# Pools laid in another order at two stage boundaries, and a last projection that ends token tile by token tile

## The chip, the cores and the metric

The kernel runs on one core of a Trainium2 chip. The metric is the device time of one execution in microseconds (us), the median of three runs.

## What is computed

Three layers with residuals over x of 512 tokens (8 batches of 64) and 512 features, all in float32. Cut to what matters:

```python
x = x + xattn(layernorm(x), ctx)      # 32 query heads, 8 key heads, 1601 keys per batch
x = x + mixer(layernorm(x))           # state space layer: 8 groups of 8 heads
x = x + routed(layernorm(x))          # top 1 of 8 experts, rank 16

# xattn: q, k rms-normed per head
out = softmax(q @ k.T * scale + mask) @ v          # per head
return out.reshape(B, Q, 32 * 128) @ o_proj_w.T    # the last projection

# mixer
dt = softplus(h @ w_dt + bias); dA = exp(-dt * exp(A_log))
xBC = silu(conv4(h @ w_in)); state = state * dA + dt * x * B; y = state @ C + x * D
return (groupnorm(y) * silu(h @ w_gate)) @ out_proj_w.T
```

## The kernel before

The work is written with tiles from pools. A pool holds so many buffers for each tag; pools are stacked in SBUF (and banks in PSUM) in the order in which they are opened, and when a stage closes its pools, the next stage's pools take the same addresses. An instruction that writes a tile waits for those that still use a pool that lay there. A scheduler orders the instructions of each engine by priority; within an engine they run in that order. All DMAs are issued by one queue, SP.

**Queries** (`project_queries`, L148). The layer norm of x, then 16 pairs of query heads in Strassen-like blocks (L199). Each quad of heads is scaled by its norm's factors (`finish`, L251, q_st) and stored to DRAM (L260, q_d). Its pools stand above the pools of context and weights: big, weights, wk2, small, late; q_raw, the factors and q_st lie in late, the topmost.

**Attention** (`attend_all`, L298). 32 units (8 batches by 4 pairs of key heads). For each unit, PE makes keys (`keys`, L375, banks a to d; evacuated into kT by ACT at L365 and DVE at L367), values (`values`, L435, into v) and, for the unit before, scores (L495), which DVE scales and masks (L500), maxima, exponentials and outputs (L565). The list `order` (L622) weaves the nine pieces of a unit's projections with the unit before's attention. Its pools are wk2, small, k, attn, v in SBUF, and two PSUM pools: ps2 with two score banks, ps1 with a, b, c, d, tr and av.

**Last projection** (`last_projection`, L669). Woven with the last unit's attention. 32 heads are taken in 16 pieces of 2; `prefetch` loads a piece's weights and attention outputs (`spare`, into the buffers of the context, a ring of four), and `piece` multiplies them for four token tiles into banks a to d (po_a to po_d). The last batches' outputs come late: for pieces 12 to 15, token tile 3 is left out (L695), and `rest` (L709) first adds po_a to po_c to x, then does these eight products for po_d with outputs loaded into o_last, and adds po_d.

**Mixer** (`mixer_and_routed`, L905). The first w_in load (L957), a layer norm with transposes for each token tile (L963, one bank px) and the products for dt (pdt, L965). A chain of small operations over [128, 256] (sp_z at L972 to a at L993) makes dt and a. For each group, `steps` (L1006, POOL) makes av from a, `decay` (L1017) multiplies it on PE (seg) and ACT takes the exponential; `project` (L1024, pj, four products for each of ten column blocks) goes through DVE's convolution (L1035, L1041) and ACT. Groups overlap: the mixing of a group (pg L1062, px, py) stands among the projections of the next. The routed layer follows at the end.

What decides the order around the change: `tc.issue_after` for ACT's table switches, the list at L1203, and else the scheduler's priorities, which by default follow the order of the text.

## Time and profile before

| what | us |
|---|---|
| median of three runs | 2874.32 (2873.58, 2874.32, 2877.37) |
| the profiled execution, its own time | 2875.87 |
| its span (first to last instruction) | 2874.1 |
| PE busy | 2815.8 |
| DVE, POOL, ACT busy | 1724.0, 834.0, 724.0 |
| first keys on PE (L375) | from 128.75 |
| first scores (L495) | from 182.77 |
| last product of the last projection (L718) | to 2345.95 |
| first projection of the mixer (L1024) | from 2356.45 |
| first mixing on PE, which begins group 1 (L1062) | 2400.66 |
| a unit of attention; a group of the mixer | 64.98; 60.1 |

How to read it: times are microseconds from the start of the span. A matmul instruction in float32 shows as two records. In a timeline row the columns are start, length, engine, line, operation, tiles, shape and count; the bracket holds the engine's idle time before the row and what ended it. PE is busy almost throughout, so the places of interest are those where it stands or where the granted TensorE clock is below 1.

### The profile page before, as it was taken

The page shows a single profiled execution, that of the slowest core. Times are in us where ns is not written, and L with a number is a line of the kernel's source. Part 1 is how long each engine was busy: PE and PEld are TensorE (multiplying, and loading weights), DVE is VectorE, ACT ScalarE, POOL GpSimd, SP SyncE. Part 2 cuts the span into 40 slices and gives each one's busy share as a digit, 9 for nine tenths or more (in the row PEclk, how much of TensorE's full clock was granted, in tenths as well). Part 3 has the DMA queues.
Part 4 walks back from the last instruction along what each step waited for, and adds up shares of the span by engine and source line. Part 5 has one row for each costly group of instructions (what it writes and reads, how often), then busy time and mean ns, then how long its engine had stood idle before and what let it go on. Part 6 is the DMA issues. An engine that isn't in the chain of part 4 may idle for free.

```text
span 2874.1 us, 37794 instructions
## 1 busy us (share of the span) xinstructions
PE 2815.8 (98%) x14716; PEld 2011.2 (70%) x14716; DVE 1724.0 (60%) x3013; ACT 724.0 (25%) x1282; POOL 834.0 (29%) x786
## 2 busy tenths in 40 slices
PE   8899999999999999999999999999999999999997
PEld 7677787777777777777777777777777544444444
DVE  4546666576667666756766676666665325445544
ACT  3222223222222222222222222222222103222221
POOL 4314323322222322232222232223222215334430
PEclk9999999999999999999999999999999999999998
DMA  4821322232113122221311222223113341121100
GB/s 162 286 61 45 85 73 52 53 93 52 45 47 93 46 63 67 73 60 45 96 49 45 66 73 60 50 68 84 46 34 89 119 160 37 52 91 64 52 15 15
DMA packets 276571, 205.89 MB, mean 72 GB/s; under 512 B 155084, under 2 KB 239882, under 8 KB 275370
## 3 DMA queue, kind: packets, MB, share of 16 engines
q1 hardware_dynamic: 276394, 203.49, 24.8%
q8 instruction: 117, 1.92, 0.3%
q14 instruction: 60, 0.49, 0.1%
HBM read 180.82 MB, written 22.62 MB: 71 GB/s over the span
## 4 chain that ended last, share of the span: by engine, by line
PE 89%; DVE 4%; DMA 3%; issue 2%; POOL 1%; ACT 0%; SPq 0%; POOLq 0%; ACTq 0%; DVEq 0%
PE pav L565 12%; PE psc L495 11%; PE pj L1024 9%; PE pv_a L435 6%; PE pv_b L435 6%; PE pv_c L435 6%; PE pk_c L375 5%; PE pk_a L375 5%; PE pk_b L375 5%; PE pv_d L435 3%; PE mo L1128 3%; PE pk_d L375 3%; PE pvl L456 2%; PE psn L404 2%; DMA nbs<-max_d 2%
## 5 line engine op out<-in xcount | busy, mean ns | idle before, releaser
L500 DVE SCALAR_TENSOR_TENSOR attn<-psc,rk,mask_sb 128x256 f32<-128x256 f32 (+1 forms) x832 | 363.7, 474 | 242.9 <-PE psc L495 225.0
L549 POOL TENSOR_TENSOR sm<-attn 128x512 f32<-128x512 f32 x64 | 81.9, 1280 | 1143.5 <-ACT attn L547 1143.5
L565 PE MATMUL pav<-attn,v 128*128 128x256 f32 (+1 forms) x1664 | 380.3, 379 | 0.0
L495 PE MATMUL psc<-q,kT 128*128 128x256 f32 x1536 | 371.2, 381 | 0.0
L552 POOL TENSOR_TENSOR sm<-sm,attn 128x512 f32<-128x512 f32 x256 | 340.0, 1328 | 29.4 <-DVE attn L543 10.7
L565 PEld LDWEIGHTS pav<-attn,v 128*128 128x128 f32 (+1 forms) x1664 | 313.9, 190 | 45.5 <-issue 1.0
L495 PEld LDWEIGHTS psc<-q,kT 128*128 128x128 f32 x1536 | 286.3, 190 | 82.0 <-issue 35.4
L1024 PE MATMUL pj<-mx_xnT,w_in 128*128 128x512 f32 x640 | 292.6, 601 | 0.0
L543 DVE TENSOR_TENSOR attn<-attn,nb 128x1024 f32<-128x1024 f32 x192 | 224.8, 1216 | 67.1 <-ACT nb L540 66.6
L435 PEld LDWEIGHTS pv_a<-wv,cx 128*128 128x128 f32 x1536 | 196.8, 192 | 58.6 <-issue 42.0
L435 PE MATMUL pv_a<-wv,cx 128*128 128x128 f32 x1536 | 214.2, 280 | 9.8 <-ACT kT L365 9.8
L547 ACT ACTIVATE attn<-attn 128x1024 f32<-128x1024 f32 x192 | 202.5, 1058 | 72.6 <-DVE attn L543 70.1
L1024 PEld LDWEIGHTS pj<-mx_xnT,w_in 128*128 128x128 f32 x640 | 118.9, 191 | 135.0 <-issue 132.9
L511 DVE TENSOR_TENSOR mx<-mx,attn 128x512 f32<-128x512 f32 x256 | 211.7, 827 | 2.0
L375 PE MATMUL pk_a<-cx,wk 128*128 128x417 f32 (+1 forms) x512 | 193.3, 500 | 0.8 <-ACT qrs L109 0.8
L386 ACT ACTIVATE ksq<-kT 128x834 f32<-128x834 f32 (+1 forms) x128 | 108.9, 871 | 161.2 <-DVE kT L367 161.2
L1132 DVE SCALAR_TENSOR_TENSOR x<-mo,rs,x 128x512 f32<-128x512 f32 x32 | 24.0, 751 | 184.6 <-PE mo L1128 184.5
L606 POOL TENSOR_TENSOR o<-o,f 128x512 f32<-128x512 f32 x31 | 39.4, 1272 | 323.7 <-DMA f<-sums_d 291.6
L375 PEld LDWEIGHTS pk_a<-cx,wk 128*128 128x128 f32 x512 | 97.2, 190 | 46.1 <-issue 20.8
L1128 PE MATMUL mo<-w_out,y 128*128 128x512 f32 x256 | 122.9, 613 | 0.0
L540 ACT COPY nb<-nbs 128x256 f32<-128x256 f32 x64 | 24.1, 376 | 324.7 <-DMA nbs<-max_d 324.7
L1041 DVE SCALAR_TENSOR_TENSOR acc<-pj,small_consts,acc 128x504 f32<-128x504 f32 x144 | 104.6, 727 | 1.0
(208 smaller groups left out, 4274.5 us busy)
## 6 DMA issues: line engine op xcount, KB each, us to landing
wk<-in_wk SPq DMA_DIRECT2D x32, 512.0 KB
wv<-in_wv SPq DMA_DIRECT2D x32, 512.0 KB
w_in<-in_w_in SPq DMA_DIRECT2D x16, 1024.0 KB
wvs<-wv_s_d SPq DMA_DIRECT2D x28, 512.0 KB
wks<-wk_s_d SPq DMA_DIRECT2D x28, 512.0 KB
cx<-in_ctxT SPq DMA_DIRECT2D x16, 834.0 KB
cx<-in_ctxT SPq DMA_DIRECT2D x16, 768.0 KB
wq<-in_wq SPq DMA_DIRECT2D x16, 512.0 KB
```

The lines of the kernel that those rows point to most:

```text
L375: nc.tensor.matmul(ps[:, :w], lhsT=u.wk[l][:, dc, :], rhs=u.cx.r[ch][r][:, dc, :], start=start and dc == 0, stop=dc == 1, skip_group_check ...
L386: nc.scalar.activation(sq[ch][:, :, half, :w], u.kT[:, :, half, lo:hi], AF.Square)
L435: nc.tensor.matmul(ps[:, i * HD : (i + 1) * HD], lhsT=u.cx.r[ch][r][:, dc, i * P : (i + 1) * P], rhs=u.wv[l][:, dc, :], start=start and i ...
L495: nc.tensor.matmul(ps[:rows, t - t2, :], lhsT=lhsT, rhs=qh, start=True, stop=True)
L500: nc.vector.scalar_tensor_tensor(out=s.at[:rows, t, :].rearrange("p (h q) -> p h q", h=GQ), in0=ps[:rows, t - t2, :].rearrange("p (h q) -> ...
L511: nc.vector.tensor_tensor(s.mx2, s.mx2, s.at[:, t2 : t2 + 2, :], ALU.max)
L543: nc.vector.tensor_tensor(at[:, k : k + 4, :], at[:, k : k + 4, :], nb.unsqueeze(1).to_broadcast([P, 4, 256]), ALU.add,)
L547: nc.scalar.activation(at[:, k : k + 4, :], at[:, k : k + 4, :], AF.Exp)
L552: nc.gpsimd.tensor_tensor(sm2, sm2, at[:, i : i + 2, :], ALU.add)
L565: nc.tensor.matmul(s.av[:, 0, :], lhsT=u.v[:rows, t, hh, :], rhs=s.at[:rows, t, :], start=t == 0, stop=t == NKT - 1,)
L1024: nc.tensor.matmul(pj, lhsT=G.w[:, dc, n, :], rhs=xnT[:, dc, :], start=dc == 0, stop=dc == DC - 1)
L1128: nc.tensor.matmul(po, lhsT=G.y[:, n, tt * P : (tt + 1) * P], rhs=G.wo[:, n, :], start=n == 0, stop=n == GC - 1,)
```

## The change

It has three parts.

Pools of attention: o, mx2, mx, nbs, sm2, sm, rbs and f move from the pool wk2, which stands below the key pool, to the attn pool above it, so that the key pool lies 18 KB lower. The two v buffers become two pools, one below attn and one above. In PSUM, tr and av move to a pool ps3 between the score banks and a to d.

Last projection: each piece multiplies all four token tiles, with o_last in place of the late outputs for tile 3 of pieces 12 to 15 (`load_newest` is called before the pieces that are left). The last two pieces are done in `rest`, token tile by token tile; after each tile's products its sum goes to x, and the scheduler's priority at that point is kept in `done`.

Mixer: the pools are opened in the order groups, weights, big; banks pj and y1 move to a pool of their own; the layer norm of token tile tt is given the priority of `done[tt]`.

```diff
 def attend_all(...):
+    vp = [ctx.enter_context(tc.tile_pool(name="xa_v0", bufs=1))]
     ap_ = ctx.enter_context(tc.tile_pool(name="xa_attn", bufs=2))
-    vp = ctx.enter_context(tc.tile_pool(name="xa_v", bufs=2))
+    vp.append(ctx.enter_context(tc.tile_pool(name="xa_v1", bufs=1)))
     ps2 = ctx.enter_context(tc.tile_pool(name="xa_ps2", bufs=2, space=PSUM))
+    ps3 = ctx.enter_context(tc.tile_pool(name="xa_ps3", bufs=1, space=PSUM))
     ps1 = ctx.enter_context(tc.tile_pool(name="xa_ps1", bufs=1, space=PSUM))
...
-        u.v = vp.tile([P, NKT, 2, HD], F32, tag="v", name="v")
+        u.v = vp[u.n % 2].tile([P, NKT, 2, HD], F32, tag="v", name="v")
...
-            psn = ps1.tile([P, 512], F32, tag="tr", name="psn")
+            psn = ps3.tile([P, 512], F32, tag="tr", name="psn")
...
-        u.o = wk2.tile([P, PQ, S], F32, tag="o", name="o")
+        u.o = ap_.tile([P, PQ, S], F32, tag="o", name="o")
...
     def last_projection():
+        def product(i, tt):
+            w, o, late = held[i]
+            for j in range(2):
+                h = 2 * i + j
+                if late and tt == NTT - 1:
+                    lhsT = newest[0][:, h - (HQ - PQ), :]
+                else:
+                    lhsT = o[:, j, tt * P : (tt + 1) * P]
+                nc.tensor.matmul(po[tt], lhsT=lhsT, rhs=w[:, j, :], start=h == 0, stop=h == HQ - 1)
+
         def piece(i):
-            w, o, late = held[i]
...
-            for j in range(2):
-                for tt in range(NTT - 1 if late else NTT):
...
+            for tt in range(NTT):
+                product(i, tt)
...
-        def rest():
+        def load_newest():
             last = loads.last_outputs()
             nc.sync.dma_start(
                 out=last.rearrange("p h (b q) -> p h b q", b=2), in_=o_d[NPR - 1][:, :, B - 2 :, :]
             )
-            for tt in range(NTT - 1):
-                add(tt)
-            for k in range(PQ):
...
-            add(NTT - 1)
+            newest.append(last)
+
+        def rest():
+            done = []
+            for tt in range(NTT):
+                for i in (HQ // 2 - 2, HQ // 2 - 1):
+                    product(i, tt)
+                nc.vector.tensor_tensor(x[:, tt, :], x[:, tt, :], po[tt], ALU.add)
+                done.append(tc.tile_snap_priority())
+            return done
...
 def mixer_and_routed(ctx, tc, c, x, done, w_in, w_out, w_ra, b_w, out):
+    grpp = ctx.enter_context(tc.tile_pool(name="mx_grp", bufs=2))
+    wst = ctx.enter_context(tc.tile_pool(name="mx_w", bufs=2))
     big = ctx.enter_context(tc.tile_pool(name="mx_big", bufs=1))
-    wst = ctx.enter_context(tc.tile_pool(name="mx_w", bufs=2))
-    grpp = ctx.enter_context(tc.tile_pool(name="mx_grp", bufs=2))
...
+    ps4 = ctx.enter_context(tc.tile_pool(name="mx_ps4", bufs=1, space=PSUM))

     def bank(tag, shape, name, bufs=1):
-        return ps.tile(shape, F32, tag=tag, name=name, bufs=bufs)
+        return (ps4 if tag in ("pj", "y1") else ps).tile(shape, F32, tag=tag, name=name, bufs=bufs)
...
-        layernorm_T(nc, c, small, ps, x, tt, xnT[:, :, tok], tag="px", bufs=2, pbufs=1, copy=nc.scalar.copy)
+        with tc.high_priority(offset=tc.tile_snap_priority() - done[tt]):
+            layernorm_T(
+                nc, c, small, ps, x, tt, xnT[:, :, tok], tag="px", bufs=2, pbufs=1, copy=nc.scalar.copy
+            )
```

More of the change, by code (lines that the diff above doesn't have):

```diff
@@ L483, in score @@
                 s.at = ap_.tile([P, NKT, 256], F32, tag="attn", name="attn")
-                s.mx2 = wk2.tile([P, 2, 256], F32, tag="mx2", name="mx2", bufs=1)
+                s.mx2 = ap_.tile([P, 2, 256], F32, tag="mx2", name="mx2", bufs=1)
             qh = u.q[:, hh * GQ : (hh + 1) * GQ, :].rearrange("p h q -> p (h q)")
@@ L516, in maxima @@
             at, lr = s.at, key_rows(NKT - 1)
-            mx = wk2.tile([P, 256], F32, tag="mx", name="mx")
+            mx = ap_.tile([P, 256], F32, tag="mx", name="mx")
             nc.vector.tensor_tensor(mx, s.mx2[:, 0, :], s.mx2[:, 1, :], ALU.max)
             nc.vector.tensor_tensor(mx[:lr], mx[:lr], at[:lr, NKT - 1, :], ALU.max)
-            tp = ps1.tile([P, 2, P], F32, tag="tr", name="mtp")
+            tp = ps3.tile([P, 2, P], F32, tag="tr", name="mtp")
             for i in range(2):
@@ L531, in maxima @@
             nc.sync.dma_start(out=row.rearrange("(i a q) -> a i q", i=2, q=32), in_=turned[0:P:32])
-            s.nbs = wk2.tile([P, 256], F32, tag="nbs", name="nbs")
+            s.nbs = ap_.tile([P, 256], F32, tag="nbs", name="nbs")
             marks["load"] = nc.sync.dma_start(out=s.nbs, in_=row.rearrange("(o q) -> o q", o=1).broadcast_to([P, 256]))
@@ L537, in softmax @@
             at, lr = s.at, key_rows(NKT - 1)
-            nb = ps1.tile([P, 256], F32, tag="tr", name="nb")
+            nb = ps3.tile([P, 256], F32, tag="tr", name="nb")
             nc.scalar.copy(nb, s.nbs)
-            sm2 = wk2.tile([P, 2, 256], F32, tag="sm2", name="sm2", bufs=1)
+            sm2 = ap_.tile([P, 2, 256], F32, tag="sm2", name="sm2", bufs=1)
             for k in range(0, NKT - 1, 4):
@@ L554, in softmax @@
             marks["exp"] = nc.scalar.activation(at[:lr, NKT - 1, :], at[:lr, NKT - 1, :], AF.Exp)
-            s.sm = wk2.tile([P, 256], F32, tag="sm", name="sm")
+            s.sm = ap_.tile([P, 256], F32, tag="sm", name="sm")
             nc.gpsimd.tensor_tensor(s.sm, sm2[:, 0, :], sm2[:, 1, :], ALU.add)
@@ L561, in outputs @@
             if part == 0:
-                s.av = ps1.tile([P, 2, 256], F32, tag="av", name="pav")
+                s.av = ps3.tile([P, 2, 256], F32, tag="av", name="pav")
             for t in range(0, 6) if part == 0 else range(6, NKT):
@@ L574, in outputs @@
                 nc.tensor.matmul(rb, lhsT=c.ones, rhs=s.sm, start=True, stop=True)
-                rbs = wk2.tile([P, 256], F32, tag="rbs", name="rbs")
+                rbs = ap_.tile([P, 256], F32, tag="rbs", name="rbs")
                 nc.vector.reciprocal(rbs, rb)
@@ L592, in sums @@
                 )
-            rbs = wk2.tile([P, 256], F32, tag="rbs", name="rbs")
+            rbs = ap_.tile([P, 256], F32, tag="rbs", name="rbs")
             nc.vector.reciprocal(rbs[:64], rb[:64])
             nc.sync.dma_start(out=u.rows.sums, in_=rbs[0:64:32])
-            u.f = wk2.tile([P, 512], F32, tag="f", name="f", bufs=1)
+            u.f = ap_.tile([P, 512], F32, tag="f", name="f", bufs=1)
             nc.sync.dma_start(
@@ L626, in attend_all @@
         u = Unit()
+        u.n = n
         u.b, u.pr = divmod(n, NPR)
@@ L669, in last_projection @@
     def last_projection():
-        po, held = [], []
+        po, held, newest = [], [], []
         def load(i):
@@ L688, in load @@
             return w, o, late
+        def product(i, tt):
[7 more added lines that the diff above has]
+                nc.tensor.matmul(po[tt], lhsT=lhsT, rhs=w[:, j, :], start=h == 0, stop=h == HQ - 1)
         def piece(i):
-            w, o, late = held[i]
             if not po:
                 po.extend(ps1.tile([P, D], F32, tag=k, name=f"po_{k}") for k in "abcd")
-            for j in range(2):
-                for tt in range(NTT - 1 if late else NTT):
-                    h = 2 * i + j
-                    nc.tensor.matmul(
-                        po[tt], lhsT=o[:, j, tt * P : (tt + 1) * P], rhs=w[:, j, :],
-                        start=h == 0, stop=h == HQ - 1,
-                    )
-        def add(tt):
-            nc.vector.tensor_tensor(x[:, tt, :], x[:, tt, :], po[tt], ALU.add)
+            for tt in range(NTT):
+                product(i, tt)
         def prefetch():
@@ L713, in rest @@
             )
-            for tt in range(NTT - 1):
-                add(tt)
-            for k in range(PQ):
-                h = HQ - PQ + k
-                nc.tensor.matmul(
-                    po[NTT - 1], lhsT=last[:, k, :], rhs=held[h // 2][0][:, h % 2, :],
-                    start=False, stop=h == HQ - 1,
-                )
-            add(NTT - 1)
-        return prefetch, [lambda i=i: (prefetch(), piece(i)) for i in range(HQ // 2)], rest
-    prefetch, last_pieces, rest = last_projection()
+            newest.append(last)
[7 more added lines that the diff above has]
+            return done
+        return prefetch, [
+            lambda i=i: (prefetch(), piece(i)) for i in range(HQ // 2 - 2)
+        ], load_newest, rest
+    prefetch, last_pieces, load_newest, rest = last_projection()
     before = divide = None
@@ L754, in attend_all @@
                 att[what]()
+        if not u:
+            load_newest()
         for piece in pieces[at:]:
@@ L757, in attend_all @@
         before = u
-    rest()
+    return rest()
 class Loads:
@@ L899, in load_mask, with mixer_and_routed @@
             nc.sync.dma_start(out=mask_sb[: KV - full * P, full, :], in_=maskT[full * P :, :])
-        attend_all(tc, c, x, loads, mask_sb, load_mask, q_d, o_d, rows_d, wo, queries_loaded)
+        return attend_all(tc, c, x, loads, mask_sb, load_mask, q_d, o_d, rows_d, wo, queries_loaded)
 @with_exitstack
-def mixer_and_routed(ctx, tc, c, x, w_in, w_out, w_ra, b_w, out):
+def mixer_and_routed(ctx, tc, c, x, done, w_in, w_out, w_ra, b_w, out):
     nc = tc.nc
+    grpp = ctx.enter_context(tc.tile_pool(name="mx_grp", bufs=2))
+    wst = ctx.enter_context(tc.tile_pool(name="mx_w", bufs=2))
     big = ctx.enter_context(tc.tile_pool(name="mx_big", bufs=1))
-    wst = ctx.enter_context(tc.tile_pool(name="mx_w", bufs=2))
-    grpp = ctx.enter_context(tc.tile_pool(name="mx_grp", bufs=2))
     wk = ctx.enter_context(tc.tile_pool(name="mx_wk", bufs=2))
@@ L1266, in perceiver @@
     c = make_consts(nc, cpool, small)
-    cross_attention(tc, c, x, ctxT, maskT, wq, wk, wv, wo)
-    mixer_and_routed(tc, c, x, w_in, w_out, w_ra, b_w, out)
+    done = cross_attention(tc, c, x, ctxT, maskT, wq, wk, wv, wo)
+    mixer_and_routed(tc, c, x, done, w_in, w_out, w_ra, b_w, out)
 def kernel(**inputs):
```

## The prediction

> **What bounds the kernel now.** I read the chain that ended last, then the timeline at the two places where one stage's pools follow another's, then the busy time by stretches there. The page's chain:

> ```profile
> PE 89%; DVE 4%; DMA 3%; issue 2%; POOL 1%; ACT 0%; SPq 0%; POOLq 0%; ACTq 0%; DVEq 0%
> ```

> The end is set by PE nearly everywhere (busy 2815.8 of 2874.1 us). So an edit counts where PE stands, runs at half clock, or gets more work. Boundary 1, from queries to attention, in the timeline:

> ```profile
> 136.27 1.63 PEld L435 LDWEIGHTS pv_d<-wvs,cs 128*128 128x128 f32 x12
> ...
> 141.84 0.36 SPq L260 DMA_DIRECT2D q_d<-q_st  x1
> ...
> 147.27 0.56 DVE L367 TENSOR_TENSOR kT<-t,pk_c 128x384 f32<-128x384 f32 x1 [5.46 <-DMA q_d<-q_st]
> 147.38 0.48 ACT L365 COPY kT<-pk_a 128x384 f32<-128x384 f32 x1 [16.51 <-DMA q_d<-q_st]
> ...
> 147.91 0.80 PE L435 MATMUL pv_a<-wv,cx 128*128 128x128 f32 x2 [9.81 <-ACT kT L365]
> ```

> The first keys stand finished in PSUM from about 134, but nobody may copy them into kT until the last queries' store, issued at 141.84, has read its tile; PE stands 9.81 us. The busy time by stretches (third to last column: the granted clock) shows what follows:

> ```profile
> 142.00:146.00 4.00, 0.00 (x0) 0.00 (x0) 0.00 (x0) 0.00 (x0) 0.00 (x0) 0.61 0.81 238
> ...
> 150.00:152.00 2.00, 2.00 (x7) 1.39 (x7) 0.56 (x1) 0.05 (x1) 1.84 (x3) 0.50 0.00 0
> ```

> The clock is halved until about 153. Boundary 2, from the last projection to the mixer:

> ```profile
> 2345.95 0.69 DVE L703 TENSOR_TENSOR x<-x,po_d 128x512 f32<-128x512 f32 x1 [3.36 <-PE po_d L718]
> ...
> 2345.99 2.54 SPq L940 DMA_DIRECT2D w_in<-in_w_in  x4
> ...
> 2346.69 0.66 PE L132 MATMUL ln_tp<-ident,ln_xn 128*128 128x128 f32 x4 [0.78 <-DVE x L703]
> ...
> 2354.69 1.97 PE L965 MATMUL pdt<-small_consts,mx_xnT 128*128 128x64 f32 x8 [0.68 <-ACT mx_xnT L133]
> 2356.45 12.18 PE L1024 MATMUL pj<-mx_xnT,w_in 128*128 128x512 f32 x22
> 2356.70 0.42 DVE L972 TENSOR_TENSOR sp_z<-pdt,small_consts 128x256 f32<-128x256 f32 x1 [6.48 <-PE pdt L965]
> ...
> 2366.89 8.04 POOL L1006 TENSOR_TENSOR av<-a,upto 128x512 f32<-128x512 f32 x8 [1.58 <-DVE a L993]
> ...
> 2368.47 3.75 PE L1017 MATMUL seg<-av,past 128*128 128x512 f32 x8
> ```

> After the last product (call T = 2345.95 its end) come four small rounds of transposes and pdt, 10.5 us, then pj. The clock is halved again from 2354.7 to 2361.5. The seg matmuls need av, which hangs on a chain over DVE, ACT and POOL; 11 pj instructions (22 records) run in front of them and hide it.

> **The change part by part.**

> *Boundary 1.* In the built program the key pool moves from bytes 143,424-170,176 of a partition, which reach into the queries' late pool (from 167,552), to 124,992-151,728, which do not. The kT writes lose their waits for the stores, and PE's order becomes pk_c, pv_a, pv_d, pv_b. From the slot at 136.59, where pv_d starts now: pk_c 1.29, pv_a 1.34, pv_d 1.34 (steps between starts at full clock), so pv_b starts at 140.56 instead of 153.15: **-12.6 us**. It is 9.8 of standing, 2.6 of half clock (5.24 us for 2.63 us of work) and 0.2 of rounding. What is late next is DVE's queue, where the two groups of q_st (L251, four of 2.74 us together) now stand between kT and v instructions. The first runs 134.8 to 137.5 (its factors landed by 134.0); then kT is written at 138.1, and pv_b, which waits for that, starts 2.5 us later. The second runs 142.6 to 145.3 (factors landed at 139.05); the v instruction behind it ends at 145.9, and pv_c's second half needs it at 146.7: 0.8 us of slack, and whatever the second group is later than that is lost. The rows from there to the first scores (psn, keys_d, rk) are released by PE, so the gain is kept; in steady state the order on every engine is unchanged and each DMA is issued behind an instruction that moves along with it.

> *The products token tile by token tile.* Their number is the same (128 of 0.86 us). The last two loads wait for products of spare 10 and 11, as now; w_ra and bw (272 and 256 KB) are put in front of them on SP; at the 385 GB/s of the rows at 2356 they take 0.7 us each, while spare 15 is first used some 15 us after its issue. Nothing.

> *Layer norms between.* 8 of the 16 transposes now stand among the po products, so they lie ahead of T, where they hide DVE and ACT. Their own time lies before T: 0.61/4 = 0.15 us each if they stream, up to 0.25 if each breaks the stream (a pdt instruction with its own load has 0.94/4 = 0.24): +1.2 to +2.0, I take **+1.4**. The norm of a tile takes 2.8 us from the end of its products (add 0.72, statistics 0.69, aggregate 0.17, two ACT steps 0.5, scale 0.55, gaps) and the next tile's four products 3.4, so no wait is added there.

> *From T to group 1.* Now: T to the first pg of group 1 at 2400.66 is 54.7 us. After, again from T: transposes 0.6, pdt of three tiles 2.8, transposes of the last 0.6, its copy 0.7, its pdt 1.1: done at 5.8. The first w_in load still waits for the last product: its pool ends up at byte 103,552, and the weight pool with o_last ends at 103,680, so 128 bytes overlap. Its part for the first pj landed 8.94 us after issue in this trace (2345.99 to 2354.89), so pj starts at 9.0, not 10.5. But only 2 pj instructions stand ahead of the seg matmuls in the new order, not 11: PE is done with them at 10.7 and must wait for av. sp_z starts at 5.9; the chain to the end of a takes 7.56 us (2356.70 to 2366.39 less three acc steps of about 1 us each that stood between, plus 0.4 and gaps); POOL's first av 1.0 (8.04/8) and 0.1: seg starts at 14.6. **PE stands 3.9 us, and behind the waiting seg stand 38 pj instructions.** Four seg at one per av end at 18.5. Then 38 pj and 4 seg of 0.858 (36.0) and 0.3: group 1 at 54.8. That is at full clock. With PE standing or lightly loaded from 5.8 to 14.6, I expect half clock there, as in both rows above, until a busy stretch has passed: at 150 it came back 5.2 us after work began. 5.1 us at half cost the seg some 2 us (1.72 each in place of 1.0): **group 1 at 56.8, +2.1**. Bounds: +0.1 (no half clock) and +3.0 (half clock for 6.8 us, the length of the one at 2354.7).

> *The clock.* The trace halves the clock at 2354.7 although no pause of PE between 2346.69 and 2356.45 is over 0.8 us: light work is enough. [...]

> *Other moves.* PSUM: the transposes' bank now lies over banks that attention has left, and pj's over the products' banks, whose last reader (DVE's add) is done 8 us before pj. w_out is scaled after the first four av: its next reader is group 1, 40 us later. Nothing.

> Sum: -12.6 + 1.4 + 2.1 = **-9.1 us**. Ends: -12.6 + 1.2 + 0.1 = -11.3 and -12.6 + 2.0 + 3.0 = -7.6. The profiled execution took 2875.87 (span 2874.1 and 1.8 around it), so 2866.8 there; the median of the runs shown is 1.55 lower, 2874.32, and gives **2865.2**.

> **The rivals.**

> 1. *The clock stays full at seg.* For it: pauses are cut by pj. Against: the 2354.7 row. -12.6 + 1.4 + 0.1: 2863.2. [...] Chance 0.22.
> 2. *Boundary 1 does not open* (the change does not do what it says): another wait holds kT or v until the store has landed. For it: q_st is still queued on DVE among them. Against: no such wait is left in the built program. Only the costs stay: 2874.3 + 3.5 = 2877.8. Chance 0.06. Something between this and the forecast (a late q_st, half clock on and on through group 0): 2867 to 2872, chance 0.08.
> 3. *Slower: a cost in every unit.* o, mx2, mx, nbs, sm and f lie at other addresses, tr and av in other banks. If each of 32 units (64.98 us each, 224.01 to 288.99 in the chain) lost 0.5 us to that, +16 - 9.1: 2881.2. It ends above no change from 0.28 us a unit. Against: the order and the number of buffers are the same. Chance 0.04.

> **How the numbers follow.** The forecast has 0.60. A measurement here tells about 0.2% (5.7 us) from no change, so "faster" is under 2868.6: forecast, rival 1 and part of the middle, 0.85; same 0.11; slower 0.04. The range takes in -11.3 and the middle case, and the runs of before, which spread from -0.7 to +3.1 about their median: 2861.5 to 2870.

> **What would show it.** Right: at about 138 us the kT rows have no wait for q_d, pv_b starts near 140.6, and the clock stays at 1.00 through 142-153; the first w_in load is still issued with the last po_d; pj comes as 4 records, then seg with a wait for POOL av of some 4 us, at half clock; the last product to the first pg of group 1 takes about 57 us. Wrong: first scores less than 12 us earlier (boundary 1), w_in issued well before the last product, or pj running while av is not there (boundary 2), units of other than 65 us (rival 3).

## The result, and the profile after

The changed kernel takes **2866.01 us** (median of 6 runs, 2864.11 to 2866.56); the kernel before took 2875.85 in the same session (6 runs, 2873.58 to 2877.91). The ratio is 0.9965, 95% interval 0.9952 to 0.9978. The profiled execution has a span of 2864.9 us (before 2874.1). Forecast: 2865.2, range 2861.5 to 2870.

The chain that ended last, on the page of the changed kernel:

```profile
PE 90%; DVE 5%; DMA 2%; issue 2%; POOL 1%; ACT 0%; SPq 0%; POOLq 0%; ACTq 0%; DVEq 0%
```

PE still sets the end. The timeline of the changed kernel at boundary 1 (line numbers are 3 higher here, 15 to 18 in the mixer):

```profile
138.00 0.55 DVE L370 TENSOR_TENSOR kT<-u,pk_b 128x384 f32<-128x384 f32 x1
138.11 0.37 SPq L260 DMA_DIRECT2D q_d<-q_st  x1
...
141.22 1.50 PE L438 MATMUL pv_b<-wvs,cs 128*128 128x128 f32 x12
...
143.24 2.73 DVE L251 SCALAR_TENSOR_TENSOR q_st<-q_raw,qw,qrsb 128x512 f32<-128x512 f32 x4
...
145.89 0.55 DVE L370 TENSOR_TENSOR v<-t,pv_c 128x384 f32<-128x384 f32 x1
```

kT is written at 138.00 without a wait for a store, while the last q_st is still to come (143.24). pv_b comes 12 us earlier; from the first key matmul (pk_a) on, 12.6. Its busy time by stretches, the same two stretches as before:

```profile
142.00:146.00 4.00, 4.00 (x37) 3.25 (x36) 3.29 (x7) 0.48 (x1) 0.00 (x0) 1.00 0.71 226
150.00:152.00 2.00, 2.00 (x7) 1.10 (x6) 0.02 (x1) 0.51 (x1) 0.00 (x0) 1.00 0.69 274
```

PE works through the first stretch (before: 0.00 of 4.00) and the clock, third from the end, is 1.00 in both. Boundary 2, the timeline of the changed kernel:

```profile
2336.58 2.50 SPq L955 DMA_DIRECT2D w_in<-in_w_in  x4
...
2336.85 2.79 PE L983 MATMUL pdt<-small_consts,mx_xnT 128*128 128x64 f32 x24
...
2342.01 0.42 DVE L990 TENSOR_TENSOR sp_z<-pdt,small_consts 128x256 f32<-128x256 f32 x1 [2.65 <-PE pdt L983]
...
2346.84 3.78 PE L1042 MATMUL pj<-mx_xnT,w_in 128*128 128x512 f32 x4 [4.92 <-DMA w_in<-in_w_in]
...
2349.61 4.04 POOL L1024 TENSOR_TENSOR av<-a,upto 128x512 f32<-128x512 f32 x4 [56.52 <-DVE a L1011]
...
2350.70 4.53 PE L1035 MATMUL seg<-av,past 128*128 128x512 f32 x8
```

T, the end of the last product, is 2336.55. The chain behind pdt starts 5 us earlier than it did, but w_in is still issued with T, so PE stands 4.92 us for it; the four pj records run at half clock (3.78 for 1.7 us of work), and seg starts as soon as av is there. The busy time of the stretch at half clock (0.50, third from the end):

```profile
2345.26:2352.09 6.83, 5.17 (x6) 2.01 (x7) 4.09 (x7) 0.00 (x0) 2.48 (x3) 0.50 1.06 379
```

Where the 9.3 us of span went, from the starts of the same instructions in both traces (us):

| stretch | before | after | difference |
|---|---|---|---|
| start to the first pk_a | 128.75 | 129.41 | +0.66 |
| first pk_a to the first mtp (L522, now L525) | 75.67 | 63.09 | **-12.58** |
| 31 units, to the last unit's first mtp | 2033.91 | 2035.54 | +1.63 |
| from there to T | 107.58 | 108.51 | +0.93 |
| T to the first pg of group 1 | 54.75 | 54.84 | +0.09 |
| from there to the last pj | 411.61 | 411.75 | +0.14 |
| from there to the end | 61.87 | 61.72 | -0.15 |

Boundary 1 gave what was forecast. The second half of the change gave nothing: it is 1 us dearer. Two rows, +0.66 and +1.63, were in no forecast; the first pk_a comes at 127.17 to 129.41 in the 13 traces of this document, whatever was changed.

### The profile page after: what moved, and what is told of

It reads as the page before. It is cut to its first block, busy times and chain, and to the rows that moved or that the text cites. A ratio compares the mean times of both kernels' runs of the same rounds, so it can differ in the third digit from the quotient of the medians.

```text
span 2864.9 us, 37796 instructions
## 1 busy us (share of the span) xinstructions
PE 2812.5 (98%) x14716; PEld 2009.4 (70%) x14716; DVE 1722.5 (60%) x3013; ACT 724.1 (25%) x1282; POOL 832.3 (29%) x786
## 4 chain that ended last, share of the span: by engine, by line
PE 90%; DVE 5%; DMA 2%; issue 2%; POOL 1%; ACT 0%; SPq 0%; POOLq 0%; ACTq 0%; DVEq 0%
PE pav L568 12%; PE psc L498 11%; PE pj L1042 9%; PE pv_a L438 6%; PE pv_b L438 6%; PE pv_c L438 6%; PE pk_a L378 5%; PE pk_c L378 5%; PE pk_b L378 5%; PE pv_d L438 3%; PE mo L1146 3%; PE pk_d L378 3%; PE pvl L459 2%; PE psn L407 2%; DMA nbs<-max_d 2%
## 5 line engine op out<-in xcount | busy, mean ns | idle before, releaser
L555 POOL TENSOR_TENSOR sm<-sm,attn 128x512 f32<-128x512 f32 x256 | 339.2, 1325 | 29.4 <-DVE attn L546 10.7
L543 ACT COPY nb<-nbs 128x256 f32<-128x256 f32 x64 | 24.1, 376 | 322.4 <-DMA nbs<-max_d 318.3
```

The costliest lines, as they stand in the source:

```text
L555: nc.gpsimd.tensor_tensor(sm2, sm2, at[:, i : i + 2, :], ALU.add)
```

## The experiments

My theory after reading this: boundary 1 earns all of it; at boundary 2 what was taken from behind T came back as a wait for w_in. The rival: av or the clock holds boundary 2, and w_in only happens to be seen. Ratios are to the kernel before on the same chip, with 95% intervals.

**The attention part alone** (e_attn_only): the diff's hunks up to `u.n = n`; last projection and mixer as before.

> The attention's pools and banks as changed; the last projection and the mixer's pools as before. Theory: the first boundary alone is worth -12.6 us (9.8 of standing, 2.6 of half clock, 0.2), and nothing else moves: 2875.9 - 12.6 = 2863.3, that is 2 to 3 us faster than the whole change (the transposes' 0.9 and the little that its second half costs). Rival, the second half is what earns a part of the gain: slower than the whole change, 2868 or more. What the trace should show: pv_b 12 us earlier, the time from the last product to the first pg of group 1 at 54 to 55 us as before.

Measured: 2865.63 (5 runs), ratio 0.9955 (0.9942 to 0.9968). In its trace pk_a to mtp takes 63.09, to the hundredth the changed kernel's; T to group 1 takes 58.36, not 54 to 55, since the clock was halved there for four windows of 3.41 us in a row (2338.5 to 2352.1). The half alone earns the whole gain. That it earns 2 to 3 us more than both halves was expected; the ratios differ that way by 0.0010 (2.9 us), but their intervals overlap, so it is not shown.

**The projection part alone** (e_proj_only): the other hunks; attention's pools and banks as before.

> The last projection, its order and the mixer's pools as changed; attention's pools and banks as before. Theory of the prediction: the first boundary stays closed (0), and the second half costs 1 to 3.5 us: 2877 to 2879. Rival, from the order of the built program: with attention's old banks no transpose stands among the products (they come after the last one), 7 pj instructions stand ahead of seg, and w_in lands about 10.3 us after the last product as in the changed kernel; then 44 instructions of 0.86 us and up to 3.4 us of half clock give group 1 at 51.8 us after the last product in place of 54.7: about 2873.

Measured: 2877.88 (11 runs), ratio 0.9999 (0.9990 to 1.0007): no gain. As the rival had it, no transpose stands among the products here, so this half's interleaving needs the pools and banks of the other. But the rival's 51.8 did not come: T to group 1 took 56.29. Most of the 4.5 us between is my count: ahead of group 1 stand 40 pj and 8 seg instructions, 48, not 44 (3.4 us). PE also stands 1.94 for av, and pj came 1.2 earlier than assumed; the two halved windows were in the 51.8 already. The same miscount is in the next two expectations that have a 44.

**128 bytes left empty** (e_gap):

```diff
     grpp = ctx.enter_context(tc.tile_pool(name="mx_grp", bufs=2))
+    gap = ctx.enter_context(tc.tile_pool(name="mx_gap", bufs=1))
+    gap.tile([P, 32], F32, name="gap")
     wst = ctx.enter_context(tc.tile_pool(name="mx_w", bufs=2))
```

> The changed kernel with 128 bytes left empty ahead of the mixer's weight pool, so that it lies over nothing of the pool of the last outputs. In the built program the first w_in load is then issued among the last loads of wo, before the last products, and 13 pj instructions stand ahead of seg. Theory: w_in's late landing (10.3 us after the last product) is what holds the stage; without it pj begins when the last tile's norm, transposes and pdt are done, 5.4 us after the last product, and PE has no reason to stand afterwards: 5.4 + 44 x 0.858 + 0.3 = 43.5 us to group 1 in place of 54.8, so 2866.0 - 11.3 = 2854.7; with half clock for 6.8 us somewhere in it 2858. Rival 1: av holds the stage as well, seg comes at 14 us whatever w_in does, and PE stands for it: not under 2863. Rival 2: the early loads (5 MB of w_in and w_out) delay the loads of wo, and the products wait for these, up to 6.9 us: 2859 to 2862.

Measured: **2857.51** (5 runs), ratio 0.9934 (0.9922 to 0.9946). SP's and PE's timeline in its trace (T is 2335.91):

```profile
2260.44 0.39 SPq L957 DMA_DIRECT2D w_in<-in_w_in  x1
```

```profile
2340.17 1.10 PE L985 MATMUL pdt<-small_consts,mx_xnT 128*128 128x64 f32 x8 [0.68 <-ACT mx_xnT L133]
2341.11 11.38 PE L1044 MATMUL pj<-mx_xnT,w_in 128*128 128x512 f32 x26
2352.71 4.13 PE L1037 MATMUL seg<-av,past 128*128 128x512 f32 x8 [0.22 <-POOL av L1026]
...
2383.56 0.34 PE L1082 MATMUL pg<-xbc 128*64 128x64 f32 x4
```

w_in is issued 75 us ahead of T, pj follows pdt without a pause, and group 1 starts at T + 47.65: 5.2 + 48 x 0.858 + 0.3 = 46.7, and 0.9 that are lost to av, by standing (0.22) and by seg's running at av's pace. That is 7.2 us less than in the changed kernel, in place of the 11.3 expected; the miscount (3.4) and av's 0.9 are the difference. Neither rival showed: no product waits for a load of wo (the stretch from the last unit's first mtp to T is 108.50), and PE does not stand for av beyond the 0.22.

What held the load back was not the overlapping bytes themselves. In the built program of the changed kernel they are the end of a weight buffer of the values (wvs), which PE read last at 2192.55, 144 us before the load was issued; o_last, which is read until T, lies 20 KB lower (bytes 79,104 to 83,200). The load, issued at 2336.58, waited for the last reader of the whole pool (T, 2336.55).

**pj ahead of seg, w_in as late as ever** (e_seg):

```diff
+    for n in (8, 9, 4):
+        ahead[0, n] = product_in(g0, n)   # project's four matmuls
     last = None
     for tt in range(NTT):
         last = decay(g0, tt)
```

> The changed kernel with the pj products of three columns of group 0 (12 instructions) put ahead of its four seg matmuls; w_in loads as late as in the changed kernel. Theory: w_in bounds the start of pj, 10.3 us after the last product, and av's chain costs only what seg loses by running at av's pace and PE at half clock meanwhile: from pj's start 44 x 0.858 + 0.3 + up to 3.4 of half clock = 41.5 in place of 44.5, so 3 us: 2863. Rival, av is the bound that counts (the prediction's 3.9 us of standing and 2.1 of half clock): 5 to 6 us, 2860. Rival 2, neither counts, the half clock moves along: 2866.

Measured: 2865.06 (6 runs), ratio 0.9952 (0.9941 to 0.9963); PE's timeline in its trace:

```profile
2346.92 13.15 PE L1043 MATMUL pj<-mx_xnT,w_in 128*128 128x512 f32 x24 [4.97 <-DMA w_in<-in_w_in]
2359.91 3.76 PE L1035 MATMUL seg<-av,past 128*128 128x512 f32 x8
```

T to group 1 is 54.66, the second rival's value: without any standing behind pj's start, the 5 us at half clock are now paid in full (12 pj in 13.0 us in place of 10.3), while in the changed kernel they fall where PE would wait for av anyway. av and the clock hide each other. This holds for the profiled execution, which was the longest of the six (2866.61); two others took 2859.9, so the step may be worth more than this execution shows.

**The changed kernel again** (e_after).

> The changed kernel once more, beside the next three on one chip. Both theories: ratio to the kernel before 0.9965 as first measured (0.9952 to 0.9978); 54.8 us from the last product to group 1; the attention stages drift by 1 to 2 us at the turns between groups of four units, in either direction. If the drift of +1.6 us seen in the first profile belonged to the change, it comes back with the same sign and at the same turns.

Measured: 2866.97 (5 runs), ratio 0.9968 (0.9956 to 0.9981). PE's timeline at boundary 2 (T is 2336.70):

```profile
2345.46 3.78 PE L1042 MATMUL pj<-mx_xnT,w_in 128*128 128x512 f32 x4 [3.40 <-DMA w_in<-in_w_in]
2350.85 5.62 PE L1035 MATMUL seg<-av,past 128*128 128x512 f32 x8 [1.61 <-POOL av L1024]
```

In this execution w_in came 1.5 us earlier, and it did not help: seg starts at T + 14.15 in both executions. Here PE stands for av in plain sight, 1.61 us, and the halved clock reaches into seg (5.45 us to the next pj, against 4.36). T to group 1: 55.92. The drift over 31 units is there again, +1.95; its cause is in the last section.

**Both v buffers in one pool at the end** (e_v_together).

```diff
-    vp = [ctx.enter_context(tc.tile_pool(name="xa_v0", bufs=1))]
     ap_ = ctx.enter_context(tc.tile_pool(name="xa_attn", bufs=2))
-    vp.append(ctx.enter_context(tc.tile_pool(name="xa_v1", bufs=1)))
+    vp = ctx.enter_context(tc.tile_pool(name="xa_v", bufs=2))
```

> The changed kernel with both v buffers in one pool at the end, as before; the first then lies over the queries' q_st and qrsb tiles, and its first write waits for the last store of q_st. Theory: kT is written as early as in the changed kernel (138 us), pv_a to pv_c run as early, but the first v instruction, at 145.9 there, waits until the store issued at 146.0 has landed (5.4 us after its issue, as at 147.27 in the kernel before): 151.4. PE runs out of free banks at about 147.6 and stands 4 us, half clock after it up to 2.6: 4 to 7 us slower than the changed kernel, 2870 to 2873, pv_b's first at 141. Rival, the keys' pool alone opened the boundary and the values follow it without loss: 2866.

Measured: 2867.72 (7 runs), ratio 0.9970 (0.9959 to 0.9981). Its timeline:

```profile
148.25 1.46 PE L497 MATMUL psc<-q,kT 128*128 128x256 f32 x6
...
149.96 0.55 DVE L369 TENSOR_TENSOR v<-t,pv_c 128x384 f32<-128x384 f32 x1 [4.70 <-DMA q_d<-q_st]
150.03 0.48 ACT L367 COPY v<-pv_a 128x384 f32<-128x384 f32 x1 [5.35 <-DMA q_d<-q_st]
150.56 0.97 PE L377 MATMUL pk_a<-cx,wk 128*128 128x417 f32 x2 [0.85 <-ACT v L367]
```

The wait is where it was expected, 4.70 us of it, but PE stands only 0.85: in this build the next keys and the first six scores stand between and fill the gap. First pk_a to first mtp takes 64.20, 1.1 more than in the changed kernel, not 4 to 7. So of the 12.6 us 1.1 hang on the values' pools, and some 11.5 on the rest of attention's change. That the rest is the keys' pool is read from the wait that went, kT's for the stores; no run takes the PSUM pools by themselves.

**Layer norms after the products** (e_norms_after, and e_gap_norms_after with the 128 bytes empty as well).

```diff
-        with tc.high_priority(offset=tc.tile_snap_priority() - done[tt]):
-            layernorm_T(
+        layernorm_T(
```

> The changed kernel without the raised priority of the layer norms: all 16 transposes come after the last product, 9 pj instructions ahead of seg; w_in is still issued with the last product. Theory: w_in holds pj until 10.3 us after the last product whatever the norms do, so what the interleaving takes from behind the last product it only turns into waiting, and its 0.9 us ahead of it is a loss: pj at 10.5, then 48 instructions of 0.858 and 0.3, and up to 3.4 of half clock: group 1 at 52.0 to 55.4 in place of 54.8, the last product 0.9 earlier: 2862 to 2866, not slower than the changed kernel. Rival, the interleaving earns the 5 us by which pdt is done earlier: 2871.

> The kernel with the 128 empty bytes, again without the raised priority of the layer norms. Theory: with w_in loaded early, the norms are what pj waits for, so here the interleaving counts: pj at 10.5 us after the last product in place of 5.2, the last product 0.9 earlier: 4.4 us slower than with the 128 bytes alone, and up to 3.4 more if the longer light stretch halves the clock: 4 to 8 us. Rival, av is the bound by then (seg at 16.8 with the gap alone, 3.5 us later at most): under 2 us slower.

Measured: 2866.4 (5 runs), ratio 0.9964 (0.9951 to 0.9976), the changed kernel's time; and with the gap 2863.3 (5 runs), ratio 0.9950 (0.9936 to 0.9964). Without the gap pj starts at T + 9.33, right behind pdt: w_in had landed by then. But T to group 1 took 57.41, not 52.0 to 55.4. What the sum left out is a wait of seg, behind 9 pj (the timeline of e_norms_after):

```profile
2357.65 5.51 PE L1032 MATMUL seg<-av,past 128*128 128x512 f32 x8 [3.41 <-POOL av L1021]
```

With the gap, pj starts at T + 11.62 (three halved windows in the light stretch) in place of 5.21, and T to group 1 is 54.95 in place of 47.65: 7.3 us lost for the 0.9 saved ahead of T. So the interleaving is worth nothing while w_in is late. Once it is early it was worth 6.4 us in these executions and 4.6 to 5.2 by the ratios. The clock has a part in that: the same norms without the gap, with one window halved, had pj at T + 9.33.

**Matmuls of no use while PE stands** (e_fill; e_seg_fill with the 12 pj ahead of seg).

```diff
+    fill = bank("y0", [P, NT], "fill")
+    for i in range(5):
+        nc.tensor.matmul(fill, lhsT=c.ident, rhs=xnT[:, i % DC, :], start=i == 0, stop=i == 4)
```

> The changed kernel with five more matmuls of 128x512 (4.3 us, their result unused) where PE stands for w_in, so that the clock need not halve; 4 pj instructions instead of 2 stand ahead of seg in the built program. Theory: av holds seg at 14.15 us after the last product in each profile of the changed kernel, so a full clock takes off only what half clock does behind that: seg at 14.15, four of 1.0, then 36 pj and 4 seg of 0.858 and 0.3: group 1 at 52.8, of which 1.7 comes from the two pj instructions that move ahead of seg and 0.3 to 1.4 from the clock; 2 to 3 us under the changed kernel, 2864. Rival (prediction): half clock alone costs 2.1 and the two moved instructions 1.7 more: 51, 2862. Rival 2, the fillers come too early or too late for the clock's window and it halves all the same: 54 to 56, 2866.

> The same five matmuls together with 12 pj instructions ahead of seg. Theory: with 12 instructions ahead and w_in at 8.8 to 10.3, nothing stands behind pj's start, so the half clock is then the only loss, 2.8 to 3.4 us in the run without the fillers (54.7 to group 1): 9 to 10.3 + 48 x 0.858 + 0.3 = 50.3 to 51.8, 3 to 4 us less than with the 12 instructions alone, 2862 to 2863. Rival, the loss is not the clock's: 54 to 55, 2865.

Measured: 2862.1 and 2862.3 (5 runs each), ratios 0.9944 (0.9930 to 0.9957) and 0.9944 (0.9931 to 0.9956). The clock stays at 1.00 through boundary 2 in both. PE's timeline of the first (T is 2334.59):

```profile
2339.79 4.51 PE L990 MATMUL fill<-mx_xnT,ident 128*128 128x512 f32 x10
2345.06 3.70 PE L1046 MATMUL pj<-mx_xnT,w_in 128*128 128x512 f32 x8 [0.76 <-DMA w_in<-in_w_in]
2348.74 4.13 PE L1039 MATMUL seg<-av,past 128*128 128x512 f32 x8
```

seg again at T + 14.15; T to group 1 is 52.73 (theory 52.8, the prediction's split 51) and 52.07 in the second (theory up to 51.8). In the second the fillers alone take 2.6 us off e_seg's 54.66: that was the clock's price there, and 4.3 us of useless work were cheaper. By the ratios both versions are some 7 us under the changed kernel (0.9944 against 0.9968); boundary 2 accounts for 2 to 3 of them. In the first profile the rest is mostly in the last row of the table (58.44 in place of 61.72).

**The 128 bytes once more** (e_gap_again).

> The 128 empty bytes alone, once more. Theory: 47.6 us from the last product to group 1 as in its first profile, no half clock there, ratio to the kernel before 0.9934 (0.9922 to 0.9946), 7 us under the changed kernel. Rival, the clock stayed full by luck the first time: up to 3.4 us more, 2861.

Measured: 2858.66 (5 runs), ratio 0.9932 (0.9920 to 0.9945); T to group 1 47.64, clock 1.00 throughout boundary 2. This is the fastest version found: 0.66% to 0.68% under the kernel before, where the changed kernel is 0.32% to 0.35% under it.

## Why the prediction was right, step by step

*Boundary 1: -12.6.* Measured -12.58, and 63.08 or 63.09 from pk_a to mtp in all ten profiles with the whole of attention's change. Mechanism, order and size held. The slack of 0.8 us behind the second q_st group was enough.

*Products tile by tile: 0.* Held: the number of products and their steps of 0.86 us are the same, and in none of the traces do they wait.

*Transposes among the products: +1.4.* Measured +0.92 or +0.93 in every profile that has them (107.58 to 108.50): 0.12 each, less than the 0.15 taken for a streaming one.

*T to group 1.* The steps at full clock held: pj at 9.0 (measured 8.8 to 10.5 from run to run where it waits for w_in, 10.3 in the first profile), seg at 14.6 (14.15 in four profiles, whatever pj did), group 1 at 54.8 without half clock (54.43 in e_v_together, whose halved windows ended before seg). The chain to the end of a took 7.52 for the forecast's 7.56, though in the kernel before four steps of acc stood in it, not three. What was mis-sized is **the half clock, +2.1**: "5.1 us at half cost the seg some 2 us". It cost 0, 0.4 and 1.5 in three profiles (e_v_together, the changed kernel, e_after), since the halved windows began while PE stood for w_in and were partly used up by the two pj instructions, which had av to wait for behind them. The 3.9 us of standing before seg were therefore seen as 0.1 and 1.6: late and slow pj filled them. The forecast's +0.1 bound is what the first profile shows, with the mechanism of the forecast and not that of rival 1: the clock did halve.

Half clock did not need PE to stand throughout: of the 3.41 us ahead of it PE was busy for a share of 0.02 in the changed kernel (from 2341.84), but of 0.61 in the kernel before (from 2351.27) and of 0.32 in the repeat (from 2340.77).

*The sum.* Predicted -9.1; the profiles differ by 9.3, the medians by 9.8. That it is so close is luck: the two costs of the second half were too dear by 0.5 and 2.0 us, and the start (+0.66) and the units (+1.63), which no step had, took 2.3 back.

*The rivals.* The first boundary opened (rival 2). The units take 64.98 us as before (rival 3). Rival 1's size came true for boundary 2, its reason did not.

*What the prediction saw and did not price:* it named the 128 bytes by which the weight pool overlaps the last outputs' pool, and went on with the late load as given. In e_gap they were worth 7.2 us, more than half of what boundary 1 gave.

## What to carry to other kernels

When pools of two stages meet, compare the byte ranges at both ends: here an overlap of 128 bytes made a load wait for the last reader of the whole pool, and a gap cost nothing. Work moved from behind a point pays only if nothing else ends there; before moving it, list what the next instruction waits for (here norms, w_in, av, clock) and how late each is, for the second latest is what remains. Two waits that lie over each other cannot be priced one at a time: in the profiled executions removing av alone gave 0.2 us, a full clock alone is worth 0.4 there, both together gave 2.8.

## What the runs showed of the hardware

Neither the busy share nor the share without the transposes tells by itself which window is followed by half clock: the one at 2351.27 of the kernel before (busy 0.61, 0.35 without its transposes) was, the one at 2345.86 of e_proj_only (busy 0.57, 0.24 without) was not.

*The drift of the units.* Seven times, where a new group of four units begins, a unit takes 66.4 to 68.1 us in place of 64.98. In all 13 traces that is 59.11 us plus the time from the start of nmt to the start of nb (L530 and L543 of the changed kernel), the maxima's way to DRAM and back, to within 0.02 us: 59.11 + 7.85 = 66.96 for the first one before. That way took 7.2 to 9.0 us there, and mostly about 5 elsewhere; below 64.98 - 59.11 = 5.87, worked out from these, it would be hidden. The last unit hangs on it too (7.56 before, 8.04 after). Together this is the +1.63: 55.42 - 54.23 + 0.48 = 1.67. So it is the latency of this way. That the change lengthens it is not shown: e_proj_only, with the attention of before, has +1.91, and the 31 units take 2033.91 to 2039.08 in the 13 traces. What lengthens it at these places was not tried.
